# Taking item 0 off a running sum: two products per step on TensorE, or eight masks per step on ScalarE

## The chip, the cores and the metric

The kernel runs on one core of a Trainium2 chip. The metric is the device time of one execution in microseconds (us). The core has five engines with a queue each: TensorE (PE in the profile; PEld is its weight load), VectorE (DVE), ScalarE (ACT), GpSimd (POOL) and SyncE (SP, which here only issues DMAs). Engines wait for each other through semaphores, and each works through its own queue in order.

## The reference

The inputs are `r_seq` (1024 users by 50 item numbers), `r_lengths` (1024), an embedding table of 100001 rows by 128 floats, and `gamma` and `beta` (128 each). Cut to what matters:

```python
emb = emb_table.at[0].set(0.0)                  # item 0 counts as nothing
e = emb[seq]                                    # 1024 x 50 x 128
prefix = jnp.cumsum(e, axis=1)
denom = jnp.minimum(t_idx[None, :], lengths[:, None])
uF = prefix / denom[:, :, None]
y = (uF - uF.mean(axis=0)) * rsqrt(uF.var(axis=0) + BN_EPS) * gamma + beta
def step(v, x):                                 # for each of the 50 steps
    v = v + (x - v) / 2.0
    spike = (v - 1.0 >= 0)
    return v - spike, spike
uF_out = spikes.mean(axis=0)                    # 1024 x 128
scores = uF_out @ emb.T                         # 1024 x 100001
```

Row 0 of the table has to be treated as zero wherever a user's sequence holds the item 0.

## The kernel before, in words

The work has two parts. The first is a loop over T = 50 steps, with the 128 features on the partitions and the 1024 users along the free dimension. The second is the product of the spike counts with the whole table; its output of 409.6 MB is stored on SP's queue.

The first part, per step t:

- **Gather** (`gather`, L204 to L212). Eight indirect DMAs on POOL fetch the rows of the table for the step's items into a tile `e` of 128 x 1024: eight blocks n of 128 users by 128 features. `e` has two buffers, so the gathers of step t+2, which are issued in step t (L332), wait until the transposes of step t have read theirs.
- **Transposes** (L319 to L329). TensorE transposes each block and adds it, in place, to a running sum in PSUM, `pre`, two halves h of 128 x 512. So `pre` is the prefix sum of the reference.
- **uF** (L330, two halves on VectorE) scales the sum by the larger of 1/(t+1) and 1/length. bn_stats (L331) and bn_aggr (L337) give mean and variance in `mv`.
- **Normalization.** ScalarE takes the square root (L341) and centres uF (L348), VectorE computes the factor `a` from four tiny instructions (L354 to L367), ScalarE applies it (`x`, L371), and VectorE adds half of the state (`step`, L374) into `v`, a PSUM tile of 128 x 1024.
- **Spikes.** `over` (L290, instruction L293) writes `d` = v - 1 on ScalarE; `rest` (L296) turns it into the reset state `negv` on VectorE in the next step, and `spiked` (L299) adds the spikes to `count`.

Item 0 is taken off as follows. Before the loop, the kernel builds `zT` (128 x 1024), which has on partition u a 1 for each user whose item at step u is 0 (`isz`, L219 to L226, transposed), twice, at u and at u + 64; and `r0n`, minus row 0 of the table, split into a high and a low part (L227 to L232). `only(t)` (L266) makes, for five steps at a time, a tile `ls` that holds r0n on the partitions of step t alone. `correct(t, l)` (L279) then adds `ls.T @ zT` to `pre`, two products of 128 x 512: for each user with item 0 in step t it subtracts row 0. The products for step t+1 are issued in step t, behind the transposes of step t and ahead of those of t+1 (L335); they wait until uF of step t has read the half. The first pair also starts the accumulation in PSUM (`start=t == 0`).

The order in each engine's queue is the order of the program, which is written by hand (`manual_schedule`). ScalarE's queue per step: square root, centring of uF, `x`, `over`. In steps 42 and 44, `prepare` (L148) also transposes and splits a piece of the table, with a copy on ScalarE (L152) and a subtraction on VectorE (L153), ahead of the second part. SP loads 40 of the table's 98 pieces at the start, during the first 50 us.

Of the kernel before, what the change touches and what calls it, by code (L numbers as in the profile page):

```python
# [12 lines left out]
F32 = mybir.dt.float32  # L13
BF16 = mybir.dt.bfloat16
F32R = mybir.dt.float32r
I32 = mybir.dt.int32
U32 = mybir.dt.uint32
AF = mybir.ActivationFunctionType
ALU = mybir.AluOpType

P = 128
# [4 lines left out]
BANK = 512  # L26
GROUP = 6
AHEAD = 6
ONLY = 5
TWICE = 2  # L30
ASIDE = 2
SHIFT = TWICE + ASIDE
# [7 lines left out]
def rec_kernel(  # L40
# [9 lines left out]
    nc = tc.nc  # L50
    B, T = seq.shape
    N, D = table.shape
    NB = B // P
# [21 lines left out]
    ident = const.tile([P, P], F32, tag="ident", name="ident")  # L75
# [96 lines left out]
    with ExitStack() as ph:  # L172
        once = ph.enter_context(tc.tile_pool(name="once", bufs=1))
        lp = ph.enter_context(tc.tile_pool(name="lif", bufs=1))
        sp = ph.enter_context(tc.tile_pool(name="stats", bufs=3))
        up = ph.enter_context(tc.tile_pool(name="uF", bufs=1))
        gp = ph.enter_context(tc.tile_pool(name="gather", bufs=2))
        accp = ph.enter_context(tc.tile_pool(name="acc", bufs=1, space=bass.MemoryType.PSUM))
        vp = ph.enter_context(tc.tile_pool(name="v", bufs=1, space=bass.MemoryType.PSUM))

        idx = once.tile([P, NB, T], I32, tag="idx", name="idx")
        nc.sync.dma_start(out=idx, in_=seq.rearrange("(p n) t -> p n t", n=NB))
        len_i = once.tile([P, NB], I32, tag="len_i", name="len_i")
        nc.sync.dma_start(out=len_i, in_=lengths.rearrange("(p n) -> p n", n=NB))
        r0 = once.tile([P, D], F32, tag="r0", name="r0")
        nc.sync.dma_start(out=r0, in_=table[0:1, :].to_broadcast([P, D]))
        gb = once.tile([P, 2], F32, tag="gb", name="gb")
        nc.sync.dma_start(out=gb[:, 0:1], in_=gamma.rearrange("(d o) -> d o", o=1))
        nc.sync.dma_start(out=gb[:, 1:2], in_=beta.rearrange("(d o) -> d o", o=1))
# [12 lines left out]
        es = {}  # L202
# [9 lines left out]
                )  # L212

        make_identity(nc, ident)
        isz = up.tile([P, NB, P], F32, tag="uF", name="isz")
        rb = up.tile([P, NB, P], F32, tag="uF", name="rb")
        gather(0)

        nc.vector.memset(isz, 0.0)  # L219
        for u in (0, P // 2):  # L220
            nc.vector.tensor_single_scalar(isz[:, :, u : u + T], idx, 0.0, ALU.is_equal)
        zps = vp.tile([P, B], F32, tag="v1", name="zps")
        for n in range(NB):
            nc.tensor.transpose(zps[:, n * P : (n + 1) * P], isz[:, n, :], ident)
        zT = once.tile([P, B], F32R, tag="zT", name="zT")
        nc.scalar.copy(zT, zps)  # L226
        r0hi = once.tile([P, D], F32R, tag="r0hi", name="r0hi")  # L227
        nc.scalar.copy(r0hi, r0)
        r0n = once.tile([P, D], F32, tag="r0n", name="r0n")
        nc.vector.tensor_scalar_mul(r0n, r0hi.bitcast(F32), -1.0)  # L230
        up2 = slice(P // 2, P)
        nc.vector.tensor_tensor(r0n[up2, :], r0hi[up2, :].bitcast(F32), r0[up2, :], ALU.subtract)  # L232
        sel = once.tile([P, P // 2], F32, tag="sel", name="sel")
        nc.vector.tensor_tensor(sel, ident[:, : P // 2], ident[:, P // 2 :], ALU.add)


        rl = once.tile([P, NB], F32, tag="rl", name="rl")
        nc.vector.tensor_copy(rl, len_i)
# [16 lines left out]
        count = once.tile([P, B], BF16, tag="count", name="count")  # L255
# [5 lines left out]

        pre = [accp.tile([P, BANK], F32, tag=f"pre{h}", name=f"pre{h}") for h in range(B // BANK)]

        ls = once.tile([P, ONLY, D], F32R, tag="ls", name="ls")

        def only(t):  # L266

            k = t % ONLY
            if k == 0:
                n = min(ONLY, T - t)  # L270
                nc.vector.tensor_tensor(
                    ls[:, :n, :],
                    r0n.unsqueeze(1).to_broadcast([P, n, D]),
                    sel[:, t : t + n].unsqueeze(2).to_broadcast([P, n, D]),
                    ALU.mult,
                )
            return ls[:, k, :]

        def correct(t, l):  # L279
            for h in range(B // BANK):  # L280
                nc.tensor.matmul(  # L281
                    pre[h],
                    lhsT=l,
                    rhs=zT[:, h * BANK : (h + 1) * BANK],
                    start=t == 0,
                    stop=False,
                    skip_group_check=True,
                )

        def over(t, v):  # L290

# [11 lines left out]
        halves = [slice(h * BANK, (h + 1) * BANK) for h in range(B // BANK)]  # L303
        v = None

        correct(0, only(0))
        l = only(1)
        gather(1)
        for t in range(T):
            last = t == T - 1  # L310
            e = es.pop(t)
            if last:
                spiked(count, whole, v)
                rest(d, v)
                near = once.tile([P, P], F32, tag="r0", name="near")
                nc.vector.tensor_scalar(near, negv[:, :P], -0.5, hgb[:, 1:2], ALU.mult, ALU.add)
            uF = up.tile([P, B], F32, tag="uF", name=f"uF_{t}")
            bs = sp.tile([P, B // BANK, 6], F32, tag="bs", name=f"bs_{t}")
            for h, cs in enumerate(halves):  # L319
                for k in range(0, BANK, P):  # L320
                    nc.tensor.matmul(  # L321
                        pre[h][:, k : k + P],
                        lhsT=e[:, h * BANK + k : h * BANK + k + P],
                        rhs=ident,
                        start=False,
                        stop=last,
                        is_transpose=True,
                        skip_group_check=True,
                    )  # L329
                nc.vector.scalar_tensor_tensor(uF[:, cs], rlen[:, cs], 1.0 / (t + 1), pre[h], ALU.max, ALU.mult)  # L330
                nc.vector.bn_stats(bs[:, h, :], uF[:, cs])  # L331
            if t + 2 < T:  # L332
                gather(t + 2)
            if not last:
                correct(t + 1, l)  # L335
            mv = sp.tile([P, 2], F32, tag="mv", name=f"mv_{t}")
            nc.vector.bn_aggr(mv, bs.rearrange("p h s -> p (h s)"))  # L337


            r = sp.tile([P, 1], F32, tag="r", name=f"r_{t}")  # L340
            nc.scalar.activation(r, mv[:, 1:2], AF.Sqrt, bias=eps)  # L341
            if last:
                centred = once.tile([P, P], F32, tag="r0hi", name="centred")
                nc.vector.tensor_scalar(centred, uF[:, :P], mv[:, 0:1], hgb[:, 2:3], ALU.subtract, ALU.mult)
                w = sp.tile([P, 1], F32, tag="w", name="w")
                nc.vector.tensor_scalar_add(w, mv[:, 1:2], BN_EPS)
            else:
                nc.scalar.activation(uF, uF, AF.Identity, bias=mv[:, 0:1], scale=-1.0)  # L348


            if t and not last:
                rest(d, v)

            nc.vector.reciprocal(r, r)  # L354
            q = sp.tile([P, 1], F32, tag="q", name=f"q_{t}")
            a = sp.tile([P, 1], F32, tag="a", name=f"a_{t}")
            if last:
                nc.vector.tensor_scalar(q, w, r, r, ALU.mult, ALU.mult)
                nc.vector.scalar_tensor_tensor(q, q, 3.0, r, ALU.subtract, ALU.mult)
                vA = once.tile([P, P], F32, tag="r0n", name="vA")  # L360
                nc.vector.scalar_tensor_tensor(vA, centred, q, near, ALU.mult, ALU.add)
                spiked(countA, slice(0, P), vA)
                nc.vector.tensor_mul(a, q, hgb[:, 0:1])
            else:
                nc.vector.scalar_tensor_tensor(q, mv[:, 1:2], BN_EPS, r, ALU.add, ALU.mult)
                nc.vector.tensor_scalar(q, q, r, 3.0, ALU.mult, ALU.subtract)
                nc.vector.tensor_scalar(a, q, r, hgb[:, 0:1], ALU.mult, ALU.mult)  # L367


            def x(vt, cs):  # L370
                nc.scalar.activation(vt, uF[:, cs], AF.Identity, bias=hgb[:, 1:2], scale=a)  # L371

            def step(vt, cs):
                nc.vector.scalar_tensor_tensor(vt, negv[:, cs], -0.5, vt, ALU.mult, ALU.add)  # L374

            if not last:
                vt = vp.tile([P, B], F32, tag=f"v{t % 2}", name=f"v_{t}")
                x(vt, whole)
                if t:
                    spiked(count, whole, v)  # L380
                step(vt, whole)
                v = vt
                d = over(t, v)
                if t + 2 < T:
                    l = only(t + 2)

                if t in (T - 8, T - 6):
                    q = (t - T + 8) // 2
                    pair(q)
                    prepare(q, vp.tile([P, HALF], F32, tag="v1", name=f"pt_{q}"))  # L390
                    if q == TWICE - 1:
                        for k in range(TWICE):
                            rows[GROUP + ASIDE + k] = first[:, k, :]
                        nc.sync.dma_start(
                            out=first[:, :TWICE, :],
                            in_=table[(GROUP + ASIDE) * HALF : (GROUP + SHIFT) * HALF, :].rearrange(
                                "(q p k) d -> p q (k d)", p=P, k=KQ
                            ),
                        )

        warm = vp.tile([P, HALF], F32, tag="v0", name="warm")
# [139 lines left out]
```

## Time and profile before

| | |
|---|---|
| median of 6 runs | 1642.99 us (1642.27 to 1647.73) |
| the profiled execution | 1647.36 us |
| its span | 1645.3 us |
| granted TensorE clock, mean | 0.797 |
| PE busy | 1081.1 us (66%) |
| DVE busy | 945.1 us (57%) |
| ACT busy | 667.7 us (41%) |
| POOL busy | 380.7 us (23%) |
| DMA | 488.12 MB, mean 297 GB/s |

The durations below come from one profiled execution. Its span runs from the first to the last instruction; 2.1 us of its time lie around it. A row of a group gives the line, the engine, the operation, the tile written and the tiles read, then the busy time and the mean of one, and behind the last bar the time that the engine stood idle ahead of such instructions and who ended it. "issue" means that nothing in the profile was waited for; "remote" is a releaser that the profile can't name. Matmuls are pipelined and their ends in the profile are modelled.

### The profile page before, as it was taken

How to read it: one execution, taken by the hardware profiler on the slowest of the kernel's cores; microseconds unless marked ns; L12 is line 12 of the kernel's file. 1: busy time of each engine (PE TensorE's matmuls, PEld its weight loads, DVE VectorE, ACT ScalarE, POOL GpSimd, SP SyncE). 2: the span in 40 equal slices, each digit the busy share in tenths (PEclk: the TensorE clock that was granted, in tenths of full speed). 3: DMA queues.
4: the chain of work that ended last, by engine and by line, in shares of the span. 5: the costliest groups of instructions: out<-in, count | busy, mean ns of one | idle time of the engine just before them, and what ended most of it. 6: DMA issues, size and time to landing. Idle time of an engine off the chain costs nothing.

```text
span 1645.3 us, 12229 instructions
## 1 busy us (share of the span) xinstructions
PE 1081.1 (66%) x4452; PEld 807.3 (49%) x4452; DVE 945.1 (57%) x1125; ACT 667.7 (41%) x697; POOL 380.7 (23%) x406
## 2 busy tenths in 40 slices
PE   4333333323333388889998888888788887888884
PEld 2112111111122266666776666666666666666663
DVE  5667656655565765666655555555545555555552
ACT  2323323322332344455544444444444444444442
POOL 7666666666666500000000000000000000000000
PEclk7555555555555599999999999999999999999998
DMA  9611111111111269999999999999999999999997
GB/s 347 235 47 47 46 45 48 46 45 47 48 49 44 64 282 416 404 421 416 404 425 426 430 429 422 425 425 425 418 428 415 416 419 425 427 417 418 426 415 335
DMA packets 51313, 488.12 MB, mean 297 GB/s; under 512 B 10079, under 2 KB 10336, under 8 KB 30004
## 3 DMA queue, kind: packets, MB, share of 16 engines
q1 hardware_dynamic: 30752, 430.86, 62.3%
q0 software_dynamic: 12800, 26.24, 5.9%
q10 hardware_dynamic: 7700, 30.23, 4.6%
q8 instruction: 35, 0.57, 0.1%
q14 instruction: 26, 0.21, 0.0%
HBM read 77.69 MB, written 409.60 MB: 296 GB/s over the span
## 4 chain that ended last, share of the span: by engine, by line
DMA 47%; DVE 17%; PE 10%; another core or an unknown queue 10%; ACT 7%; issue 4%; POOL 3%; ACTq 0%; DVEq 0%; SPq 0%; POOLq 0%
DMA scores<-o 46%; PE po L160 9%; ACT o L504 5%; POOL e L207 3%; DVE bs L331 3%; DVE uF L330 3%; DVE v L374 3%; DVE negv L297 2%; DVE count L300 2%; DVE o L502 1%; DMA e<-in_L_rec_emb_table,idx 1%; ACT v L371 1%; ACT uF L348 1%; DVE a L367 1%
## 5 line engine op out<-in xcount | busy, mean ns | idle before, releaser
L502 DVE TENSOR_SCALAR o<-po 128x1024 f32<-128x1024 f32 x391 | 464.1, 1221 | 345.7 <-DMA scores<-o 310.6
L504 ACT ACTIVATE o<-po 128x1024 f32<-128x1024 f32 (+1 forms) x391 | 388.8, 1018 | 542.3 <-DMA scores<-o 328.4
L207 POOL DMA_INDIRECT e<-in_L_rec_emb_table,idx x400 | 380.0, 950 | 185.0 <-issue 115.2
L160 PE MATMUL po<-pairs,countB 128*128 128x512 f32 (+1 forms) x1120 | 295.1, 410 | 66.4 <-ACT o L504 51.5
L160 PEld LDWEIGHTS po<-pairs,countB 128*128 128x128 f32 x1120 | 212.3, 195 | 129.5 <-ACT o L504 68.7
L281 PE MATMUL pre<-zT,ls 128*128 128x512 f32 x100 | 78.7, 789 | 296.1 <-DVE uF L330 233.9
L160 PE MATMUL po<-pairs,countC 128*128 128x512 f32 (+1 forms) x840 | 230.9, 423 | 45.8 <-ACT o L504 45.6
L160 PEld LDWEIGHTS po<-pairs,countC 128*128 128x128 f32 x840 | 164.9, 203 | 92.2 <-ACT o L504 57.5
L281 PEld LDWEIGHTS pre<-zT,ls 128*128 128x128 f32 x100 | 29.1, 293 | 335.5 <-DVE uF L330 260.8
L330 DVE SCALAR_TENSOR_TENSOR uF<-rlen,pre 128x512 f32<-128x512 f32 x100 | 68.0, 680 | 175.1 <-remote 159.3
L321 PE MATMUL pre<-ident,e 128*128 128x128 f32 x400 | 120.2, 433 | 65.4 <-DMA e<-in_L_rec_emb_table,idx 44.0
L153 DVE TENSOR_TENSOR pairs<-pt,pairs 128x1024 fp32r<-128x1024 f32 x70 | 84.6, 1217 | 89.7 <-ACT pairs L152 89.7
L321 PEld LDWEIGHTS pre<-ident,e 128*128 128x128 f32 x400 | 81.1, 211 | 105.5 <-DMA e<-in_L_rec_emb_table,idx 66.4
L341 ACT ACTIVATE r<-mv,eps 128x1 f32<-128x1 f32 x50 | 14.8, 295 | 290.2 <-DVE mv L337 183.1
L136 PE MATMUL pt<-ident,rows 128*128 128x128 f32 (+1 forms) x768 | 108.9, 289 | 10.0 <-issue 4.9
L136 PEld LDWEIGHTS pt<-ident,rows 128*128 128x128 f32 (+1 forms) x768 | 98.8, 152 | 27.9 <-issue 12.6
L160 PE MATMUL po<-hi,countB 128*128 128x512 f32 x208 | 86.4, 416 | 16.1 <-ACT o L504 10.9
L160 PE MATMUL po<-lo,countB 128*128 128x512 f32 x208 | 83.6, 402 | 0.0
L293 ACT ACTIVATE d<-v,less 128x1024 bf16<-128x1024 f32 x49 | 54.5, 1113 | 63.6 <-DVE v L374 36.3
L160 PE MATMUL po<-pairs,countA 128*128 128x512 f32 x280 | 70.1, 395 | 11.0 <-ACT o L504 11.0
L152 ACT CAST pairs<-pt 128x1024 fp32r<-128x1024 f32 x70 | 70.6, 1008 | 16.3 <-PE pt L136 16.3
L160 PE MATMUL po<-hi,countC 128*128 128x512 f32 x156 | 66.3, 425 | 13.5 <-ACT o L504 13.4
(85 smaller groups left out, 870.1 us busy)
## 6 DMA issues: line engine op xcount, KB each, us to landing
scores<-o SPq DMA_DIRECT2D x96, 3072.0 KB
scores<-o SPq DMA_DIRECT2D x32, 1536.0 KB
scores<-o SPq DMA_DIRECT2D x30, 1024.0 KB
rows<-in_L_rec_emb_table ACTq DMA_DIRECT2D x19, 1536.0 KB
scores<-o SPq DMA_DIRECT2D x8, 2896.5 KB
rows<-in_L_rec_emb_table SPq DMA_DIRECT2D x5, 3072.0 KB
e<-in_L_rec_emb_table,idx POOLq DMA_INDIRECT x400
rows<-in_L_rec_emb_table SPq DMA_DIRECT2D x2, 1024.0 KB
```

The lines of the kernel that those rows point to most:

```text
L136: nc.tensor.transpose(pt[:, k0 : k0 + pw], r[:pw, k0 : k0 + D], ident[:pw, :pw])
L152: nc.scalar.copy(vh, vp)
L153: nc.vector.tensor_tensor(vl, vp, vh.bitcast(F32), ALU.subtract)
L160: nc.tensor.matmul(po[:, :kw], lhsT=counts[n], rhs=part[:, k0 : k0 + kw], start=j == 0, stop=j == 1,)
L207: nc.gpsimd.indirect_dma_start(out=es[t][:, n * P : (n + 1) * P], out_offset=None, in_=table, in_offset=bass.IndirectOffsetOnAxis(ap=idx[: ...
L281: nc.tensor.matmul(pre[h], lhsT=l, rhs=zT[:, h * BANK : (h + 1) * BANK], start=t == 0, stop=False, skip_group_check=True,)
L293: nc.scalar.activation(d, v, AF.Identity, bias=less)
L321: nc.tensor.matmul(pre[h][:, k : k + P], lhsT=e[:, h * BANK + k : h * BANK + k + P], rhs=ident, start=False, stop=last, is_transpose=True, ...
L330: nc.vector.scalar_tensor_tensor(uF[:, cs], rlen[:, cs], 1.0 / (t + 1), pre[h], ALU.max, ALU.mult)
L331: nc.vector.bn_stats(bs[:, h, :], uF[:, cs])
L502: nc.vector.tensor_scalar_mul(o[:, h0 : h0 + hw], po[:, :hw], 1.0 / T)
L504: nc.scalar.mul(o[:, h0 : h0 + hw], po[:, :hw], 1.0 / T)
```

## The change

The products, and all that was built for them, are gone. A tile `some` holds 1 where a user's item is above 0, and 0 where it is 0. Once a block is gathered, ScalarE multiplies each of its rows (one user per partition) by that user's 0 or 1, in place, and the transposes then read the masked block. The eight multiplications for step t+1 are issued at the end of step t, on ScalarE behind `over` of step t and, in steps 42 and 44, behind the copy of `prepare`. Two products of zeros before the loop start the accumulation.

```diff
-        r0 = once.tile([P, D], F32, tag="r0", name="r0")
-        nc.sync.dma_start(out=r0, in_=table[0:1, :].to_broadcast([P, D]))
...
-        isz = up.tile([P, NB, P], F32, tag="uF", name="isz")
         rb = up.tile([P, NB, P], F32, tag="uF", name="rb")
         gather(0)
 
-        nc.vector.memset(isz, 0.0)
-        for u in (0, P // 2):
-            nc.vector.tensor_single_scalar(isz[:, :, u : u + T], idx, 0.0, ALU.is_equal)
-        zps = vp.tile([P, B], F32, tag="v1", name="zps")
-        for n in range(NB):
-            nc.tensor.transpose(zps[:, n * P : (n + 1) * P], isz[:, n, :], ident)
-        zT = once.tile([P, B], F32R, tag="zT", name="zT")
-        nc.scalar.copy(zT, zps)
...
+        some = once.tile([P, NB, T], F32, tag="some", name="some")
+        nc.vector.tensor_single_scalar(some, idx, 0.0, ALU.is_gt)
...
-        def only(t):
...
-        def correct(t, l):
-            for h in range(B // BANK):
-                nc.tensor.matmul(
-                    pre[h],
-                    lhsT=l,
-                    rhs=zT[:, h * BANK : (h + 1) * BANK],
-                    start=t == 0,
-                    stop=False,
-                    skip_group_check=True,
-                )
+        def masked(t):
+
+            for n in range(NB):
+                part = es[t][:, n * P : (n + 1) * P]
+                nc.scalar.activation(part, part, AF.Identity, scale=some[:, n, t : t + 1])
...
-        correct(0, only(0))
-        l = only(1)
+        for h in range(B // BANK):
+            nc.tensor.matmul(
+                pre[h],
+                lhsT=count[:, :P],
+                rhs=count[:, h * BANK : (h + 1) * BANK],
+                start=True,
+                stop=False,
+                skip_group_check=True,
+            )
+        masked(0)
         gather(1)
         for t in range(T):
...
             if t + 2 < T:
                 gather(t + 2)
-            if not last:
-                correct(t + 1, l)
...
                 d = over(t, v)
-                if t + 2 < T:
-                    l = only(t + 2)
-
                 if t in (T - 8, T - 6):
...
+                masked(t + 1)
```

More of the change, by code (lines that the diff above doesn't have):

```diff
@@ L28 @@
 AHEAD = 6
-ONLY = 5
 TWICE = 2
@@ L214, in rec_kernel @@
         make_identity(nc, ident)
-        isz = up.tile([P, NB, P], F32, tag="uF", name="isz")
         rb = up.tile([P, NB, P], F32, tag="uF", name="rb")
         gather(0)
-        nc.vector.memset(isz, 0.0)
-        for u in (0, P // 2):
-            nc.vector.tensor_single_scalar(isz[:, :, u : u + T], idx, 0.0, ALU.is_equal)
-        zps = vp.tile([P, B], F32, tag="v1", name="zps")
-        for n in range(NB):
-            nc.tensor.transpose(zps[:, n * P : (n + 1) * P], isz[:, n, :], ident)
-        zT = once.tile([P, B], F32R, tag="zT", name="zT")
-        nc.scalar.copy(zT, zps)
[L227 to L234, printed above, removed]
+        some = once.tile([P, NB, T], F32, tag="some", name="some")
+        nc.vector.tensor_single_scalar(some, idx, 0.0, ALU.is_gt)
         rl = once.tile([P, NB], F32, tag="rl", name="rl")
@@ L262, in rec_kernel @@
         pre = [accp.tile([P, BANK], F32, tag=f"pre{h}", name=f"pre{h}") for h in range(B // BANK)]
-        ls = once.tile([P, ONLY, D], F32R, tag="ls", name="ls")
-        def only(t):
[L268 to L275, printed above, removed]
-                )
-            return ls[:, k, :]
-        def correct(t, l):
-            for h in range(B // BANK):
-                nc.tensor.matmul(
-                    pre[h],
-                    lhsT=l,
-                    rhs=zT[:, h * BANK : (h + 1) * BANK],
-                    start=t == 0,
-                    stop=False,
-                    skip_group_check=True,
-                )
+        def masked(t):
+            for n in range(NB):
+                part = es[t][:, n * P : (n + 1) * P]
+                nc.scalar.activation(part, part, AF.Identity, scale=some[:, n, t : t + 1])
         def over(t, v):
```

## The prediction

> **What bounds the kernel now.** I read the busy table by slices first: for the first third of the span (0 to about 583 us, the 50 steps) the DMA engines are nearly idle, for the rest they are 90% busy storing scores. The chain of work that ended last says the same of the second part, and has one entry that belongs to the first:
>
> ```profile
> DMA 47%; DVE 17%; PE 10%; another core or an unknown queue 10%; ACT 7%; issue 4%; POOL 3%; ACTq 0%; DVEq 0%; SPq 0%; POOLq 0%
> ```
>
> The program runs on one core, so 10% of the span (165 us) has no releaser that the profile knows. The change touches only the steps; the second part should keep its length and start earlier or later. So I cut the groups of instructions to the steps (60 to 580 us, different shapes apart):
>
> ```profile
> line engine op names shapes xcount | busy us, mean ns | idle before us <-releasers
> L207 POOL DMA_INDIRECT e<-in_L_rec_emb_table,idx x360 | 340.7, 946 | 170.9 <-issue 103.6 <-remote 43.7 <-PE pre L281 21.8
> ...
> L330 DVE SCALAR_TENSOR_TENSOR uF<-rlen,pre 128x512 f32<-128x512 f32 x93 | 63.2, 680 | 163.2 <-remote 159.3 <-PE pre L321 3.0 <-issue 0.6
> ```
>
> Three rates can be read off. **Gathers:** one is 0.95 us and 0.30 us of issue, 8 a step, so 8 x 1.25 = 9.98 us a step is the floor that POOL sets. **Arithmetic:** the time order of VectorE for a step that waits for nothing:
>
> ```profile
> 244.04 0.68 DVE L330 SCALAR_TENSOR_TENSOR uF<-rlen,pre 128x512 f32<-128x512 f32 x1
> ...
> 250.25 1.23 DVE L374 SCALAR_TENSOR_TENSOR v<-negv,v 128x1024 f32<-128x1024 f32 x1 [0.21 <-issue]
> 251.39 0.68 DVE L330 SCALAR_TENSOR_TENSOR uF<-rlen,pre 128x512 f32<-128x512 f32 x1
> ```
>
> From the first half's uF to the next step's, 7.35 us. **What really happens:** uF of step 4 starts at 66.27 us and of step 49 at 578.21, so 511.9 / 45 = 11.38 us a step, 1.4 us above the gather floor. The difference sits in the 159.3 us that uF waits for "remote". One such wait, TensorE's rows first, then VectorE's:
>
> ```profile
> 214.99 0.47 PE L321 MATMUL pre<-ident,e 128*128 128x128 f32 x1 [0.70 <-issue]
> 216.21 0.48 PE L321 MATMUL pre<-ident,e 128*128 128x128 f32 x1 [0.75 <-DMA e<-in_L_rec_emb_table,idx]
> 226.38 0.79 PE L281 MATMUL pre<-zT,ls 128*128 128x512 f32 x1 [9.70 <-DVE uF L330]
> ```
>
> ```profile
> 225.64 0.69 DVE L330 SCALAR_TENSOR_TENSOR uF<-rlen,pre 128x512 f32<-128x512 f32 x1 [9.99 <-remote]
> ```
>
> By the rows the eight transposes of step 18 are over at 216.7, yet VectorE gets leave at 225.6. Matmul ends are modelled; I read this as TensorE's completions coming late. Such spells come every four or five steps, around the steps in which transposes are let go one by one by landing gathers (the two rows above, 1.2 us apart). After a spell the gathers are ahead, three steps run at 7.35 us, TensorE catches up with the gathers again and the next spell follows. That is my reading, not something the profile states.
>
> **The change part by part.** *Gone from VectorE and TensorE:* 100 products of 0.79 us, all between uF and the next transposes, off the path; ten builds of ls (0.82 us), which lengthen one step in five; the opening (isz, zps, zT, r0), which lies under the first gather (3.5 to 13.4 us, landed at 18). All at nothing, since the new order makes something else late: *the eight masks on ScalarE.*
>
> No row shows ScalarE scaling a 128x128 block by a per-row operand. The nearest have a per-row operand, SBUF to SBUF, at other widths, or the width without the operand:
>
> ```profile
> L410 ACT ACTIVATE uF<-uF,mv 128x512 f32<-128x512 f32 x1 | 0.7, 705 | 0.0
> ...
> L410 ACT ACTIVATE uF<-uF,mv 128x384 f32<-128x384 f32 x1 | 0.6, 598 | 0.0
> L228 ACT CAST r0hi<-r 128x128 fp32r<-128x128 f32 x1 | 0.3, 301 | 0.0
> ```
>
> 128 columns cost 107 ns, so 598 - 2 x 107 = 384 ns for 128. How near they follow each other, and what they stand behind, is in ScalarE's time order:
>
> ```profile
> 247.04 0.29 ACT L341 ACTIVATE r<-mv,eps 128x1 f32<-128x1 f32 x1 [1.76 <-DVE mv L337]
> 247.24 1.13 ACT L348 ACTIVATE uF<-uF,mv 128x1024 f32<-128x1024 f32 x1
> 249.01 1.21 ACT L371 ACTIVATE v<-uF,hgb,a 128x1024 f32<-128x1024 f32 x1 [0.64 <-DVE q L366]
> 251.52 1.11 ACT L293 ACTIVATE d<-v,less 128x1024 bf16<-128x1024 f32 x1 [1.30 <-issue]
> ```
>
> The second starts 0.20 us after a first of 0.29, so 0.09 overlaps and masks come every 0.29 us. Masks of step t+1 are queued behind d of step t (over), which waits for v. Before, transposes of t+1 ran under the arithmetic of t, and d lay beside uF; now nothing covers d, four masks and a transpose. Counted from 244.04: v ends at 7.44, d runs 7.48 to 8.59, mask 1 starts at 8.50, mask 4 ends at 8.50 + 3 x 0.29 + 0.38 = 9.75, its transpose (0.48, with 0.04 to hand over) at 10.28, uF starts at **10.31**. The second half: mask 8 ends at 10.91, its transpose at 11.44, before uF's second half is due at 10.31 + 1.32 = 11.63. So the arithmetic goes from 7.35 to 10.31 us a step, now just above the 9.98 of the gathers. POOL then waits for the transposes (buffer free), its gathers start as soon as transposes of t end and land some 11.2 us later (8.7 to the last issue, 2.5 to landing), while the masks want them 18 us later: neither ScalarE nor TensorE is let go by a landing any more, except in the opening.
>
> Bounds of a mask: at 301 ns, every 0.21 us, uF starts at 9.97, so the gathers bind at 9.98; at 598 ns without overlap mask 8 ends at 13.3, uF is in effect at 12.5. I take 384: it has the operand and its slope.
>
> *Where the rest goes.* Opening: the first table load now stands behind the first landing (1.28 us, from 0.74 before) and lies under the later landings. Steps 0 to 3 follow the gathers, which land late under the loads; step 4 begins at 59.4 if step 3 has no late spell (last transpose at 49.5 plus mask, 50.4, plus 9.0), at about 69 if it keeps the one it has now. I take 64. The two steps with prepare put a copy (1.01 us) ahead of the masks and may keep the 4.9 us that TensorE waits for issue there: 5 us in all.
>
> **Sum.** 64 + 45 x 10.31 + 5 = 533 us for uF of step 49, against 578.2: 45 us less. The profiled execution took 1647.4 us (span 1645.3 and 2.1 around it), so 1602; it is 4.4 us over the median of the six runs, so a median is between 1598 and 1602. I say 1600. Break-even is at (578.2 - 64 - 5) / 45 = 11.3 us a step.
>
> [...]
>
> **Rivals.** *(1) Gathers bind, no spells:* masks cheap, 9.98 a step, 59 + 449 + 2 = 510, about 68 us less: 1577 to 1580. For it: 301 ns at the same shape. *(2) The spells stay* (slower): TensorE is still let go block by block, by ScalarE, and its completions still come late. If the excess over the floor (1.4 us a step) stays on top of 10.31, 11.7 a step, 596, 18 us more: 1662. If all 159.3 us in 46 steps (3.5 a step) come on top, 13.8 a step, 111 us more: 1755. Decides from 11.3 a step, one us of delay on TensorE per step. For it: I can't say what a spell is; one begins near 284 us although most transposes of that step ran in a burst. Against: they come when landing gathers let transposes go, which ends. *(3) Masks dear:* each with a wait of its own, every 0.6 us, 12.5 a step, 53 us more: 1696. Against: the waits are long satisfied, and other ScalarE instructions follow each other without a gap.
>
> **Chances.** Forecast and its surroundings (10.1 to 11.2 a step, 1585 to 1635) 0.52; rival 1 0.06; within 0.2%, about what a measurement can tell from no change, 0.05; rival 2 0.27, rival 3 0.10. So faster 0.58, same 0.05, slower 0.37. The likeliest alone spans 1580 to 1635. The range goes to 1700: rival 2 in its milder half and rival 3 at its price; left out are about 0.04 below and 0.15 above.
>
> **What would show it.** Right: uF's remote wait nearly gone; a step of 10.3 us; uF waiting for TensorE's transpose or ScalarE's mask; POOL waiting a few tenths a step for TensorE; masks of 0.38 us, 0.29 apart. Wrong: remote waits of 5 to 13 us, masks over 0.45 us apart, masks that wait for landings after step 5, or a second part of another length.

## The result, and the profile after

The changed kernel takes **1650.3 us** (median of 17 runs, 1649.7 to 1651.4). The kernel before, run beside it, takes 1643.1 us (38 runs). The ratio is 1.0041, 95% interval 1.0032 to 1.0050: 7 us slower, where 43 us less had been forecast.

The profiled execution took 1650.15 us. From its page, the chain of work that ended last and the row of the granted TensorE clock:

```profile
PEclk9999999999999999999999999989989999999998
...
DMA 46%; DVE 16%; PE 13%; ACT 11%; issue 9%; another core or an unknown queue 3%; POOL 0%; ACTq 0%; DVEq 0%; SPq 0%
```

The unnamed releaser has fallen from 10% to 3% of the span; ScalarE (from 7% to 11%), TensorE (from 10% to 13%) and "issue" (from 4% to 9%) have taken its place. The forecast had uF's remote wait nearly gone; of 159.3 us, 43.5 are left. The groups of the steps (60 to 580 us, shapes apart) for the same instructions as before, and the masks:

```profile
L204 POOL DMA_INDIRECT e<-in_L_rec_emb_table,idx x360 | 339.6, 943 | 171.8 <-issue 103.9 <-remote 53.1 <-PE pre L290 9.3
L249 ACT ACTIVATE e<-e,some 128x128 f32<-128x128 f32 x365 | 111.3, 391 | 0.0
L299 DVE SCALAR_TENSOR_TENSOR uF<-rlen,pre 128x512 f32<-128x512 f32 x91 | 62.1, 683 | 169.5 <-PE pre L290 120.2 <-remote 43.5 <-issue 5.8
```

Read the last row against its counterpart. uF's idle time is 169.5 us where it was 163.2. Its remote wait shrank by 116 us, and the wait for the transposes (L290, which now stand behind d and the masks) grew from 3 to 120 us in its place. One was exchanged for the other almost to the microsecond. POOL's busy and idle times hardly differ at all. That is the result in two rows: an idle time changed its name.

The steps themselves show how. The order of time on ScalarE, for one step:

```profile
244.42 1.21 ACT L338 ACTIVATE v<-uF,hgb,a 128x1024 f32<-128x1024 f32 x1 [0.64 <-DVE q L333]
246.93 1.11 ACT L254 ACTIVATE d<-v,less 128x1024 bf16<-128x1024 f32 x1 [1.30 <-issue]
247.94 2.44 ACT L249 ACTIVATE e<-e,some 128x128 f32<-128x128 f32 x8
```

Eight masks in 2.44 us, 0.29 us apart, right behind d. And the uF rows of VectorE, over four steps:

```profile
226.08 0.69 DVE L299 SCALAR_TENSOR_TENSOR uF<-rlen,pre 128x512 f32<-128x512 f32 x1 [2.88 <-PE pre L290]
...
230.43 0.69 DVE L299 SCALAR_TENSOR_TENSOR uF<-rlen,pre 128x512 f32<-128x512 f32 x1 [2.92 <-remote]
...
239.44 0.69 DVE L299 SCALAR_TENSOR_TENSOR uF<-rlen,pre 128x512 f32<-128x512 f32 x1 [2.88 <-PE pre L290]
...
249.77 0.69 DVE L299 SCALAR_TENSOR_TENSOR uF<-rlen,pre 128x512 f32<-128x512 f32 x1 [2.88 <-PE pre L290]
...
260.11 0.69 DVE L299 SCALAR_TENSOR_TENSOR uF<-rlen,pre 128x512 f32<-128x512 f32 x1 [2.88 <-PE pre L290]
```

From 239.44 to 249.77 and on to 260.11 a step takes 10.33 us; the forecast was 10.31. But the step that began at 226.08 took 13.36: its second half (230.43) waited 2.92 us for "remote", though by TensorE's rows all eight transposes were over at 227.2. This happens in every third step, hardly varying, from step 6 to step 39. POOL pauses in the same place, after every 24 gathers:

```profile
225.90 0.95 POOL L204 DMA_INDIRECT e<-in_L_rec_emb_table,idx  x1 [0.30 <-issue]
230.66 0.94 POOL L204 DMA_INDIRECT e<-in_L_rec_emb_table,idx  x1 [3.82 <-remote]
231.91 0.95 POOL L204 DMA_INDIRECT e<-in_L_rec_emb_table,idx  x1 [0.31 <-issue]
```

Two steps of 10.33 and one of 13.36 make a mean of 11.34. Over all, uF of step 4 starts at 69.0 us and uF of step 49 at 581.4, so a step takes **11.386 us** on the average. Before, with an arithmetic 3 us shorter, it was 11.377. The second part kept its length (from uF of step 49 to the end of the execution 1068.7 us, 1069.1 before).

So the question for the experiments was: why does a step take 11.38 us, whether its arithmetic needs 7.35 us or 10.33?

### The profile page after: what moved, and what is told of

Same layout as the page of the kernel before. It is cut to its first block, busy times and chain, and to the rows that moved or that the text cites. A ratio compares the mean times of both kernels' runs of the same rounds, so it can differ in the third digit from the quotient of the medians.

```text
span 1648.4 us, 12524 instructions
## 1 busy us (share of the span) xinstructions
PE 1021.4 (62%) x4346; PEld 772.0 (47%) x4346; DVE 937.6 (57%) x1110; ACT 784.3 (48%) x1095; POOL 378.4 (23%) x406
## 4 chain that ended last, share of the span: by engine, by line
DMA 46%; DVE 16%; PE 13%; ACT 11%; issue 9%; another core or an unknown queue 3%; POOL 0%; ACTq 0%; DVEq 0%; SPq 0%
DMA scores<-o 46%; PE po L159 9%; ACT o L468 5%; DVE uF L299 4%; DVE bs L300 4%; PE pre L290 3%; ACT v L338 3%; DVE negv L258 2%; ACT d L254 2%; DVE v L341 2%; DVE o L466 1%; DVE count L261 1%; ACT uF L315 1%; PE pt L135 1%
## 5 line engine op out<-in xcount | busy, mean ns | idle before, releaser
L290 PE MATMUL pre<-ident,e 128*128 128x128 f32 x400 | 127.6, 476 | 426.0 <-ACT d L254 261.0
L290 PEld LDWEIGHTS pre<-ident,e 128*128 128x128 f32 x400 | 73.0, 182 | 481.4 <-ACT d L254 269.5
L249 ACT ACTIVATE e<-e,some 128x128 f32<-128x128 f32 x400 | 122.7, 391 | 4.5 <-DMA e<-in_L_rec_emb_table,idx 4.4
L159 PE MATMUL po<-hi,countC 128*128 128x512 f32 x156 | 65.8, 422 | 13.9 <-ACT o L468 13.8
L338 ACT ACTIVATE v<-uF,hgb,a 128x1024 f32<-128x1024 f32 x49 | 59.2, 1207 | 30.9 <-DVE a L334 12.8
```

Source lines behind the costliest of these rows:

```text
L159: nc.tensor.matmul(po[:, :kw], lhsT=counts[n], rhs=part[:, k0 : k0 + kw], start=j == 0, stop=j == 1,)
L249: nc.scalar.activation(part, part, AF.Identity, scale=some[:, n, t : t + 1])
L290: nc.tensor.matmul(pre[h][:, k : k + P], lhsT=e[:, h * BANK + k : h * BANK + k + P], rhs=ident, start=False, stop=last, is_transpose=True, ...
```

## The experiments

Two theories. **Cause:** something in the arithmetic or in the way TensorE is let go makes completions late, another thing in each kernel, and the equal means are chance. **Floor:** while the gathers run at 1.25 us each, a debt builds up that late completions pay off, so that a gather costs some 1.42 us in the long run. One division goes with it that I had not made: from gather 40 to gather 320 the kernel before takes 1.418 us per gather, the changed one 1.410; eight of them are 11.34 and 11.28 us. By itself it shows no floor: gathers wait for the transposes of two steps earlier, so over a long stretch their pace is the pace of the steps, whatever sets it. What speaks for a floor is that the two kernels agree though their arithmetic doesn't; the runs test that.

The table sums up what the runs gave. "Arithmetic" is the step that waits for nothing; "mean" is from uF of step 4 to uF of step 49, over 45, in the profiled execution; "remote" is uF's idle time from 60 to 560 us that ended so. The kernels with no gathers, half the gathers, half the bytes and half the rows (e2, e3, e6, e8, e10) were run once each. The 38 runs of the kernel before lie between 1639.3 and 1648.9 us, which is 0.2 us for each of 50 steps, so a difference of 0.1 or 0.2 us between two means of one execution says little.

| kernel | gathers a step | arithmetic, us | mean, us | uF's remote, us | total, us |
|---|---|---|---|---|---|
| before | 8 | 7.35 | 11.377 | 152.1 | 1643.1 |
| changed | 8 | 10.33 | 11.386 | 40.6 | 1650.3 |
| e1_mask_first | 8 | 7.95 | 11.399 | 123.7 | 1648.0 |
| e2_after_no_gather | 0 | 10.33 | 10.415 | 0 | 1596.2 |
| e3_before_no_gather | 0 | 7.35 | 7.741 | 0 | 1469.8 |
| e4_after_paced | 8, and 8 memsets on POOL | 10.33 | 11.588 | 29.0 | 1652.7 |
| e5_neither | 8 | 7.35 | 11.306 | 110.5 | 1638.3 |
| e6_before_half | 4 | 7.35 | 7.740 | 0 | 1472.5 |
| e7_before_tiny | 8 | 10.29 | 12.583 | none | 1720.3 |
| e8_before_narrow | 8, of half the bytes | 7.35 | 11.323 | 134.2 | 1651.9 |
| e9_before_long | 8 | 10.13 | 11.380 | 18.8 | 1650.5 |
| e10_before_64rows | 8, of half the rows | 7.35 | 11.393 | 160.2 | 1654.7 |

### The masks ahead of d

The eight masks stand behind x, ahead of `over`, in place of behind `over` and `prepare`.

```diff
+                masked(t + 1)
                 d = over(t, v)
...
-                masked(t + 1)
```

> The masks of step t+1 stand ahead of d of step t on ScalarE, so the arithmetic of a step should fall from 10.33 to about 9.2 us, under the 9.98 of the gathers. Theory F (a floor of about 11.35 us a step on the average of 8 gathers and the transposes behind them, paid by late completions of TensorE, whoever waits): a step stays at 11.3 to 11.4 on the mean, spells come at longer intervals but last longer, total within 5 us of the changed kernel. Theory S (a spell is a fixed price of about 3 us each 24 gathers, on top of arithmetic or gathers): 9.98 + 1.0 = 11.0 a step, 17 us less than the changed kernel. Theory L (only a chase after landings brings spells): long spells return, as before the change.

Measured: 1647.95 us, ratio to the kernel before 1.0023 (1.0007 to 1.0040). The arithmetic fell to 7.95 us, further than expected, because the masks now follow ScalarE's x at once and no longer wait for v on VectorE. Nothing of the 2.4 us came through: 11.399 us a step. The groups of the steps:

```profile
L299 DVE SCALAR_TENSOR_TENSOR uF<-rlen,pre 128x512 f32<-128x512 f32 x92 | 62.8, 683 | 161.1 <-remote 129.7 <-issue 26.4 <-PE pre L290 5.1
```

The 120 us of waiting for transposes are gone, and the remote wait is back at 129.7. The steps now come as 7.95, 7.96, 19.0, 10.2 us, over and over, 45.1 for four. What the arithmetic gives, the next spell takes. A fixed price for each spell on top of the gathers would have given 11.0 us a step.

### No gathers, in both kernels

```diff
+        kept = {}
...
         def gather(t):
+            if t > 1:
+                es[t] = kept[t % 2]
+                return
             es[t] = gp.tile([P, B], F32, tag="e", name=f"e_{t}")
+            kept[t] = es[t]
```

> The changed kernel with gathers in steps 0 and 1 only; later steps mask and transpose the same two tiles again (so the sums are of the wrong items; everything but POOL's and the DMAs' work is there). Theories F and S: spells need gathers in flight, so each step takes 10.33 us, uF of step 49 at about 30 + 48 x 10.33 = 526 plus 5 for the steps with prepare, 50 us less. Rival T (TensorE or the program makes the late completions itself, every 24 transposes): every third step still 13.4 us, time as the changed kernel's.

> The kernel before with gathers in steps 0 and 1 only (sums of the wrong items). Theories F and S: 7.35 us a step without a late completion, 7.5 with the build of ls, uF of step 49 at about 30 + 48 x 7.5 + 8 = 400, 180 us less than before. Rival T: spells of 20 us every four steps remain, 11.4 a step.

Measured: 1596.2 us for the changed kernel, 1469.8 for the one before. uF's rows in the groups (60 to 400 us), of the changed kernel without gathers:

```profile
L304 DVE SCALAR_TENSOR_TENSOR uF<-rlen,pre 128x512 f32<-128x512 f32 x66 | 44.8, 679 | 95.0 <-PE pre L295 95.0
```

and of the kernel before without gathers:

```profile
L335 DVE SCALAR_TENSOR_TENSOR uF<-rlen,pre 128x512 f32<-128x512 f32 x88 | 59.4, 675 | 0.0
```

No remote wait is left in either: the late completions belong to the gathers. And the difference between the two kernels comes to light: 126 us, most of it the 3 us a step that the masks add to the arithmetic (less the builds of ls, which lengthen one step in five from 7.35 to 8.08 us in the kernel before). In the full kernels the gathers cover it.

### A slower POOL

A memset of 128x64 (0.17 us on the mean) behind each gather, in the changed kernel, so that POOL issues a gather every 1.28 us in place of 1.25, with one more instruction for each.

```diff
+        pace = once.tile([P, 64], F32, tag="pace", name="pace")
...
+                nc.gpsimd.memset(pace, 0.0)
```

> The changed kernel with a small memset on POOL behind each gather (0.1 to 0.2 us), so that 8 gathers take 11 to 11.5 us instead of 9.98. Theory F: what was paid in spells is now paid between gathers; late completions get rare, total within 8 us of the changed kernel. Theory S: the spell each 24 gathers comes on top, 1 us more a step than POOL's own, about 12.3 a step, 45 us more.

Measured: 1652.7 us, ratio 1.0053 (1.0035 to 1.0071), 11.588 us a step. The pace was not what had been expected: 8 x 1.28 is 10.3 us, not 11 to 11.5, because most of the memset fits into the 0.30 us that lay between two gathers anyway. So a debt could still build up, and a fixed price of 1 us a step on top of 10.33 would have given 11.33 us, not far off; it is the masks ahead of d that speak against such a price. uF's remote waits fell further (29.0 us), and POOL's own memsets became late as well (26.4 us of remote waits from 60 to 560 us). In the order of time of POOL:

```profile
233.21 0.15 POOL L211 MEMSET pace<- 128x64 f32 x1 [0.61 <-remote]
233.51 0.95 POOL L205 DMA_INDIRECT e<-in_L_rec_emb_table,idx  x1
234.63 0.15 POOL L211 MEMSET pace<- 128x64 f32 x1 [0.17 <-POOL pace L211]
234.93 0.95 POOL L205 DMA_INDIRECT e<-in_L_rec_emb_table,idx  x1
236.06 0.15 POOL L211 MEMSET pace<- 128x64 f32 x1 [0.18 <-POOL pace L211]
236.37 0.95 POOL L205 DMA_INDIRECT e<-in_L_rec_emb_table,idx  x1
```

The three gathers start 1.42 and 1.44 us apart: in such stretches something near the pace of the floor shows on POOL itself, from one gather to the next. They are few; of the 310 gathers from the 40th on, 223 start about 1.28 us after the last one. Still, it isn't TensorE alone that is late: who is late depends on the program.

### Neither products nor masks

The changed kernel with both calls of `masked` taken out.

```diff
-        masked(0)
...
-                masked(t + 1)
```

> The changed kernel without its eight masks a step, so neither the two products nor the masks are there; it leaves out taking item 0 off the sums (item 0 counts like any other). A step's arithmetic should be some 7.4 us, as in the kernel before, since nothing stands between v and the next transposes. Floor theory (while gathers run, some 1.42 us per gather on the average whatever the arithmetic is): 11.3 to 11.5 us a step, the total within 5 us of the kernel before (1638 to 1650). Theory that each kernel has its own reason to be late (the old products on TensorE in the one, the masks in the other): without both, the gathers' issue binds at 9.98 us a step, 1580 to 1590.

Measured: 1638.3 us, ratio 0.9979 (0.9961 to 0.9996), 11.306 us a step. The groups of the steps:

```profile
L298 DVE SCALAR_TENSOR_TENSOR uF<-rlen,pre 128x512 f32<-128x512 f32 x92 | 62.6, 680 | 148.5 <-remote 118.0 <-PE pre L289 18.7 <-issue 11.6
```

With no work for item 0 at all, the kernel is 0.2% faster than before. That is about the most that another way to take item 0 off could win here as long as a step keeps its eight gathers, and it speaks against the theory of a cause in the products or in the masks: with neither, the spells are there.

### Half the gathers

```diff
+        kept = {}
...
-            es[t] = gp.tile([P, B], F32, tag="e", name=f"e_{t}")
-            for n in range(NB):
+            if t > 1:
+                es[t] = kept[t % 2]
+            else:
+                es[t] = kept[t] = gp.tile([P, B], F32, tag="e", name=f"e_{t}")
+            for n in range(NB if t < 2 else 4):
```

> The kernel before with four gathers a step in place of eight from step 2 on (they write half of a block that is kept; it leaves out the other rows, so its sums are of wrong items). Floor theory: four gathers need 4 x 1.42 = 5.7 us, below the arithmetic of 7.35 to 7.7 us, so no late spells, a mean step of about 7.7 us as without gathers, 1465 to 1475. Theory that any steady gathering makes TensorE's completions late: spells stay, and a step takes 9 us or more, 1530 or over.

Measured: 1472.5 us, 7.740 us a step, the same as with no gathers at all (7.741). The groups of the steps:

```profile
L211 POOL DMA_INDIRECT e<-in_L_rec_emb_table,idx x170 | 160.7, 945 | 164.2 <-PE pre L325 134.9 <-issue 29.0 <-PE pre L285 0.3
L334 DVE SCALAR_TENSOR_TENSOR uF<-rlen,pre 128x512 f32<-128x512 f32 x90 | 60.7, 675 | 0.0
```

A gather takes as long as ever (945 ns), and no uF waits for a late completion. POOL now waits for TensorE's reads (134.9 us), so it has pauses of its own; I read this as no debt building up. Gathering alone doesn't make completions late: four gathers in 7.74 us don't, eight at 1.25 us each do.

### Half the bytes, half the rows

Gathers of 64 floats a row, and gathers of 64 rows, both from step 2 on into kept blocks as above.

```diff
+            wd = D if t < 2 else D // 2
+            rows_of = table.rearrange("n (h d) -> (n h) d", d=wd)
...
-                    out=es[t][:, n * P : (n + 1) * P],
+                    out=es[t][:, n * P : n * P + wd],
...
-                    in_=table,
+                    in_=rows_of,
```

```diff
+            rows = P if t < 2 else P // 2
...
-                    out=es[t][:, n * P : (n + 1) * P],
+                    out=es[t][:rows, n * P : (n + 1) * P],
...
-                    in_offset=bass.IndirectOffsetOnAxis(ap=idx[:, n, t : t + 1].bitcast(U32), axis=0),
+                    in_offset=bass.IndirectOffsetOnAxis(ap=idx[:rows, n, t : t + 1].bitcast(U32), axis=0),
```

> The kernel before with gathers that fetch half the width from step 2 on (64 floats a row in place of 128; as many gathers and as many rows; it leaves out half of each row, so its sums are wrong). If the floor goes by gathers or by rows: still 11.3 to 11.5 us a step, 1638 to 1650. If it goes by bytes: half of 11.4 is below the issue of 9.98, so 9.98 us a step without spells, 1575 to 1590.

> The kernel before with gathers of 64 rows in place of 128 from step 2 on (as many gathers, half the rows; the other rows of a block stay as they were, so the sums are of wrong items). If the floor goes by gathers: still 11.3 to 11.5 us a step, 1638 to 1650. If it goes by rows: 64 rows need 0.7 us, below the 1.25 us of the issue, so 9.98 us a step or less, no late spells, 1590 or less.

Measured: 1651.9 and 1654.7 us, 11.323 and 11.393 us a step. Both totals lie a little above the range that I gave; the steps lie where they were expected, and step 4 begins later (72.1 us in both, 66.3 before). Half the bytes, or half the rows, in as many gathers, leave the floor where it was: it goes by the number of gathers, not by their bytes or rows.

### More instructions, or longer ones

24 memsets of one column on VectorE in each step of the kernel before, and then, in a second kernel, four long instructions that take about as much time in all.

```diff
+        tiny = once.tile([P, 1], F32, tag="tiny", name="tiny")
...
+                for _ in range(24):
+                    nc.vector.memset(tiny, 0.0)
```

```diff
+        seen = once.tile([P, 6], F32, tag="seen", name="seen")
...
+                for k in range(4):
+                    nc.vector.bn_stats(seen, negv[:, k % 2 * BANK : (k % 2 + 1) * BANK])
```

> The kernel before with 24 more instructions a step on VectorE, each a memset of one column that nothing reads. At some 0.07 us each they add 1.5 to 2 us to a step's arithmetic, which makes it 9 to 9.4 us, still below 11.4. If the floor belongs to the gathers alone: 11.3 to 11.5 us a step, the total within 5 us of the kernel before. If the floor is a rate of all instructions together (something that each instruction fills and that drains at a fixed rate): a step becomes longer than 11.6 us, the total more than 12 us over the kernel before.

> The kernel before with four long instructions a step on VectorE (bn_stats of 512 columns, some 0.69 us each, whose result nothing reads) in place of the 24 short memsets: about the same time on VectorE, 2.8 us, and so the same arithmetic of some 10.1 us a step, with a sixth of the instructions. If the 24 memsets cost 1.2 us a step because each is one more instruction to be completed while gathers run: here 11.3 to 11.5 us a step, the total within 8 us of the kernel before. If they cost it because VectorE was 2.9 us longer: 12.4 to 12.7 us a step, the total some 60 us over it, though the changed kernel, as long, does not show that.

Measured: with the 24 memsets 1720.3 us, ratio 1.0498 (1.0445 to 1.0551), 12.583 us a step; with the four long ones 1650.5 us, ratio 1.0057 (1.0035 to 1.0078), 11.380 a step. The memsets start 0.12 us apart where nothing holds them, nearly twice what I had assumed, so the arithmetic was 10.29 us and not 9 to 9.4; the second kernel, with 10.13, is the comparison that counts. The same length in four instructions costs nothing in the steps, in 24 it costs 1.2 us a step. Each memset writes the same column as the one before it, and the rows name that one as what is waited for; whether 24 memsets of different columns would cost as much wasn't tested. In the order of time of VectorE, in a spell of the first:

```profile
114.55 0.06 DVE L386 MEMSET tiny<- 128x1 f32 x1 [1.34 <-DVE tiny L386]
115.27 0.06 DVE L386 MEMSET tiny<- 128x1 f32 x1 [0.65 <-DVE tiny L386]
115.97 0.06 DVE L386 MEMSET tiny<- 128x1 f32 x1 [0.64 <-DVE tiny L386]
117.35 0.06 DVE L386 MEMSET tiny<- 128x1 f32 x1 [1.33 <-issue]
118.06 0.06 DVE L386 MEMSET tiny<- 128x1 f32 x1 [0.65 <-DVE tiny L386]
118.77 0.06 DVE L386 MEMSET tiny<- 128x1 f32 x1 [0.65 <-DVE tiny L386]
```

An instruction of 0.06 us follows the last one after 0.70 or 1.40 us: in this spell the memsets come in steps of 0.70 us. Twice that is close to the 1.42 us of a gather; whether the two hang together isn't shown. TensorE's lateness has the same step, which can be read from how long uF's second half waits for "remote" in the kernel with half the rows:

```profile
315.04 0.69 DVE L336 SCALAR_TENSOR_TENSOR uF<-rlen,pre 128x512 f32<-128x512 f32 x1 [2.83 <-remote]
...
475.19 0.69 DVE L336 SCALAR_TENSOR_TENSOR uF<-rlen,pre 128x512 f32<-128x512 f32 x1 [3.55 <-remote]
...
507.75 0.69 DVE L336 SCALAR_TENSOR_TENSOR uF<-rlen,pre 128x512 f32<-128x512 f32 x1 [1.45 <-remote]
...
555.52 0.69 DVE L336 SCALAR_TENSOR_TENSOR uF<-rlen,pre 128x512 f32<-128x512 f32 x1 [2.13 <-remote]
```

These waits, 1.45, 2.13, 2.83 and 3.55 us, are 0.68 to 0.72 us apart; a few others (1.78, 3.87) lie between. With the 24 memsets it is VectorE that is late (uF has no remote wait), as it was TensorE in the kernel before and both TensorE and POOL in the paced one. The four long instructions take 0.69 us each, as long as one such step, and wait 13.8 us in all:

```profile
L386 DVE BATCH_NORM_STATS2 seen<-negv 128x6 f32<-128x512 f32 x184 | 127.5, 693 | 13.8 <-DVE seen L386 8.8 <-issue 0.7
```

The second kernel has a further use. It keeps the products, has no masks, and has nearly the arithmetic of the changed kernel. Its total, 1650.5 us, is the changed kernel's 1650.3. So masks aren't needed for 7 us more. But that the longer arithmetic costs them isn't shown either: the kernel with the masks ahead of d has 7.95 us and takes 1647.95, where the kernel before, run beside it, took 1642.3.

## Why the prediction was wrong

- **The gather floor** is the step that failed: "Gathers: one is 0.95 us and 0.30 us of issue, 8 a step, so 8 x 1.25 = 9.98 us a step is the floor that POOL sets". 1.25 us is the pace of a burst. Sustained, a gather takes 1.41 to 1.42 us (an eighth of a mean step), and the floor is 11.3 to 11.4 us a step: that of before, of the changed kernel, and of five more with arithmetic from 7.35 to 10.13 us. The 1.4 us a step that I put down as a loss above the floor were the floor.
- **The late spells** failed with it: they come "around the steps in which transposes are let go one by one by landing gathers". In the changed kernel nothing is let go by a landing after the opening, as forecast, and completions are late all the same. The number of gathers decides whether there are spells (none with no gathers or half of them), and 24 memsets lengthen them; it doesn't matter who lets TensorE go. The observation was right that after a spell three steps run free; but with eight gathers a step no kernel here kept that pace. I read it so that they use up in advance what the next spell takes back.
- **The new arithmetic** was right to 0.02 us: 10.31 forecast, 10.33 measured. So were the masks: 384 ns forecast, 391 measured, 0.29 us apart in both, queued behind d.
- **What the arithmetic is worth** followed from the two steps above. 3 us a step more, under a floor of 11.38, vanish from the mean step; without gathers they cost most of 126 us. In my sum 10.31 stood above the floor of 9.98 and set the step; it lies below the true one.
- **The opening:** step 4 began at 69.0, the upper end of the forecast (59.4 to 69), because a late completion of 7.0 us stayed in the opening, now in step 2. Across the kernels with eight gathers the place of step 4 went from 64.1 to 72.1 us with no clear relation to the arithmetic, and to 83.9 with the 24 memsets.
- **The steps with prepare** add 3.0 us over 10.33 in the changed kernel without gathers, and the way into the last step another 0.9; 5 had been put down.
- **The second rival** had the right mechanism's outline, "the spells stay", and the wrong price. It put the excess of 1.4 us a step, or of 3.5, on top of the new arithmetic (11.7 or 13.8 us a step). The runs show that the excess fills up to a fixed pace: 4.0 us a step above an arithmetic of 7.35, 1.1 above 10.33.
- **Masks on VectorE** in place of ScalarE could hardly have paid: no run here puts them there, but the kernel with neither products nor masks still takes 11.31 us a step. **The clock** does not set the pace either: from 60 to 580 us it was granted at 1.00 after, and at 0.50 before (0.54 from 500 to 540 us), with 11.386 and 11.377 us a step.

The remaining 7 us: 3.2 of them stand in the profiles at uF of step 49 (581.4 to 578.2), of which 2.8 are already there at step 4. The rest isn't located, since the profiled execution of the kernel before was itself 4.3 us over its median.

## What to carry to other kernels

Before a gap between a pace of instructions and a pace of steps is called a loss, divide the time of a long stretch, free and late cycles together, by the count of the suspected instruction, and then change the work beside it. One steady number isn't a floor yet, since instructions that wait for each step keep the pace of the steps, whatever sets it; it is one when it stays while the work beside it grows or shrinks (here 11.3 to 11.4 us a step at an arithmetic of 7.35 to 10.33), and goes when the instruction goes. The stage under this floor was hardly made faster by less work on other engines, or slower by more of it, up to the floor: the kernel with 3 us more a step took 7 us more in all, and leaving the work out altogether won 0.2%. But 24 short instructions more did raise the step by 1.2 us. What helped was fewer gathers (in kernels that leave rows out); gathers of half the bytes or half the rows did not help. Whether fewer and larger gathers could fetch the same rows at the lower price wasn't tested.

## What the runs showed of the hardware

- A gather by an indirect DMA on POOL is issued every 1.25 us in a burst and every 1.40 to 1.43 us over 280 gathers where a step has eight of them, with 64 or 128 rows and with 256 or 512 bytes a row (1.54 beside the 24 memsets).
- With eight gathers a step (not with four), while they run at 1.25 to 1.28 us each, completions of instructions become late: TensorE's transposes (uF's waits for them 1.45, 2.13, 2.83 or 3.55 us), VectorE's 0.06 us memsets (0.70 or 1.40 us apart), POOL's memsets (gathers then 1.42 us apart). In the first two the step is 0.70 us. What decides which engine is late is open.
- 24 short memsets on VectorE raised the floor by 1.2 us a step (0.05 each). For 8 memsets on POOL (0.2 us a step by one execution, 2.3 us in all by the medians) and 8 masks on ScalarE (0.08 us a step by one execution, 12 us in all by the medians, against the kernel with neither) the scatter is too large to give a price.
- What makes these steps of 0.70 us isn't shown by any run. Every execution here left records of its span and clock, so whether the floor is there in an execution that nothing records is open too; no run tests it.
- The granted clock and the time are not tied in this kernel: runs of the unchanged kernel with a mean clock of 0.795 and 0.943 took 1639.1 and 1642.1 us.
